# Adding a scan's states with identity matmuls, with GpSimd's products later and its decays in SBUF

## The chip, the cores and the metric

The kernel runs on one core of a Trainium2 chip. Its time is the device time of one execution in microseconds (us). Five engines work side by side, each through its own queue in order: TensorE (PE, whose weight loads are shown apart as PEld), VectorE (DVE), ScalarE (ACT), GpSimd (POOL) and SyncE (SP), which here issues most transfers. SBUF is the working memory; PSUM is a small memory of eight banks, into which PE writes its results, and which ACT and DVE can read and write[...].

## What is computed

Four layers are applied to x of shape (4, 384, 48, 48), each as x + layer(group norm of x). Layer 0 is a state-space block over the 2304 positions of each image, layers 1 to 3 are a patchwise transform with a depthwise convolution, an 11x11 depthwise convolution and a mixture of four experts. The change lies in layer 0:

```python
dt, Bm, Cm = jnp.split(x_dbl, [DT_RANK, DT_RANK + D_STATE], axis=-1)
dt = jax.nn.softplus(dt @ dt_proj_w.T + dt_proj_b)
A = -jnp.exp(A_log)

def step(h_prev, inp):
    x_t, dt_t, B_t, C_t = inp
    dA = jnp.exp(dt_t[..., None] * A)
    dBx = dt_t[..., None] * B_t[:, None, :] * x_t[..., None]
    h_new = dA * h_prev + dBx
    y_t = jnp.einsum('bds,bs->bd', h_new, C_t)
    return (h_new, y_t)
...
y = ys.transpose(1, 0, 2) + xin * D
y = y * jax.nn.silu(z)
out = y @ out_proj_w.T
```

There are 768 channels (d) and 16 states (s) for each. So y of a channel is a sum over 16 states, plus the skip term xin * D.

## The kernel before

**Tiling.** Channels lie on the 128 partitions: six tiles m = 0 to 5, taken in three pairs p. Positions of an image are cut into five chunks of 460 or 464. The smallest piece of work is a *unit*: one channel tile m, one state s, one chunk. A pair has 32 units, q = 0 to 31, the two tiles of the pair in turn, so q = 2s + m%2. There are 4 x 5 x 3 = 60 pairs and 1920 units.

**A unit** (unit(), L613 on). ACT computes the decays da = exp(dt * A) (L627) into one of two PSUM banks, tag da. POOL computes bu = u * B (L631), u being dt * x, into one of three SBUF buffers. DVE runs the recurrence along the chunk in one instruction, tensor_tensor_scan (L635), from da and bu. ACT copies the last column to carry (L640), where the next chunk's scan of the same unit starts. The states are multiplied with C (L642), and PE adds the product g to y (turned(), L591).

Two kinds of unit differ in where the scan writes. In two of three units it overwrites da in PSUM, and DVE makes the product g. In the third (q divisible by 3, 11 of a pair's 32, 660 in all) it writes into g in SBUF, and POOL makes the product in place; here these are called *Pool's units*. There are four g buffers.

**Adding up.** turned() adds g to y with four transposes by PE, each of a quarter of the columns: y stands in PSUM transposed, positions on the partitions. skip() (L604 on) begins each y: ACT computes dx = xc * D (L611) into a g buffer, and four transposes put it into y's bank. There is one bank for the even tile of a pair and one for the odd (tags y0, y1). After the pair, collect() copies y to SBUF (yt, L651) by ACT; gate(), called after units 3 and 6 of the next pair, turns yt back with four transposes into a bank pyb (L659), and DVE multiplies that with the gate silu(z) (zs, L663).

**Order.** scans() is a generator that issues units one after another, and after each unit the pieces planned for it (plan(q, piece)): the projections of the next chunk (project, project_z, expand, steps), gate, and the output projection, layer norm and residual of the chunk before (tail()). While image b is scanned, work of layers 1 to 3 for the images before it (later(), experts()) is dealt out among the units at an even rate. The instructions of each engine are then ordered by priority, which follows the order of issue, and by when their inputs and buffers are free by the compiler's own estimate; so two scans may stand in front of the first one's product. A tile's tag with bufs=n has n buffers; an instruction that needs a buffer waits until its last reader is done. Layer 0's units end at about 4920 us; the last image's layers 1 to 3 follow.

**PSUM.** Tags mm (2 banks), da (2), y0, y1 and two banks for the background work make eight.

Of the kernel before, what the change touches and what calls it, by code (L numbers as in the profile page):

```python
# [9 lines left out]
F32 = mybir.dt.float32  # L10
AF = mybir.ActivationFunctionType
ALU = mybir.AluOpType
# [4 lines left out]
P = 128  # L17
# [4 lines left out]
DI, DS, DTR, DCONV = 768, 16, 24, 4  # L22
MT = DI // P
CHUNKS = (460, 460, 460, 460, 464)
TM = max(CHUNKS)
TT = 4
# [18 lines left out]
def tile_layers(ctx: ExitStack, tc: tile.TileContext, a: dict, out: bass.AP):  # L45
    nc = tc.nc
# [16 lines left out]
    def column(ap):  # L63
        return ap.rearrange("(m p) -> p m", p=P)

    ident = const("ident", [P, P], a["c_ident"])
# [197 lines left out]
    with ExitStack() as first:  # L264
        wp = first.enter_context(tc.tile_pool(name="weights", bufs=1))
# [3 lines left out]
        def weight(name, shape, src):  # L269
            t = wp.tile(shape, F32, name=name)  # L270
            nc.scalar.dma_start(t, src)
            return t
# [18 lines left out]
        nc.vector.tensor_scalar_mul(a_neg, a_neg, -1.0)  # L291
        w_out0 = weight("w_out0", [P, MT, C], per_channel(a["L0_out_proj_wT"]))
        d_col = weight("d_col", [P, MT], column(a["L0_D"]))
        gamma = weight("gamma", [P, CT], column(a["L0_ln_gamma"]))
        beta = weight("beta", [P, CT], column(a["L0_ln_beta"]))
        carry = wp.tile([P, MT, DS], F32, name="carry")
# [26 lines left out]
        with (  # L323
# [4 lines left out]
            for ct in range(CT):  # L328
                t = pp.tile([P, HW], F32, name=f"x0_{ct}")
# [65 lines left out]
        def after(ins, other):  # L395

            tc.add_manual_dep(
                ins.ins, other.ins.name,
                mybir.DependencyInfo(
                    mybir.DependencyClass.NoSync, mybir.DependencyReason.DATA  # L400
                ),
                reason="order",
            )
# [7 lines left out]
        def scans(wk, mm):  # L411


            def bank(name):
                return mm.tile([P, 512], F32, name=name, tag="mm")
# [168 lines left out]
                    )  # L584
                    nc.gpsimd.tensor_mul(u[:, h, :n], dt[:, h, :n], c["xc"][:, 2 * p + h, :n])

            def turned(y, src, n, start, stop):

                w = n // TT
                for k in range(TT):  # L590
                    nc.tensor.matmul(  # L591
                        y[:w, bass.ts(k, P)],
                        lhsT=src[:, bass.ts(k, w)],
                        rhs=ident,
                        is_transpose=True,
                        start=start and k == 0,
                        stop=stop,
                        skip_group_check=True,
                    )

            def skip(i, p):

                (b, t), c = G[i], st[i]
                n = CHUNKS[t]  # L604
                for h in range(2):
                    m = 2 * p + h
                    y = c["y", m] = mm.tile(
                        [P, 512], F32, name=f"y{b}_{t}_{m}", tag=f"y{h}", bufs=1
                    )
                    dx = wk.tile([P, TM], F32, name=f"dx{b}_{t}_{m}", tag="g", bufs=4)  # L610
                    nc.scalar.activation(  # L611
                        dx[:, :n], c["xc"][:, m, :n], AF.Copy, scale=d_col[:, m : m + 1]
                    )  # L613
                    turned(y, dx, n, True, False)

            def unit(i, m, s):

                (b, t), c = G[i], st[i]
                n, p = CHUNKS[t], m // 2
                if m % 2 == 0:  # L620
                    bc = wk.tile([P, 2, TM], F32, name=f"bc{b}_{t}_{p}_{s}", tag="bc", bufs=4)
                    c["bct"] = bc
                    nc.sync.dma_start(bc[:, :, :n], c["bc"][:, s, :n].partition_broadcast(P))
                bc = c["bct"]
                v_ = f"{b}_{t}_{m}_{s}"
                da = mm.tile([P, 512], F32, name=f"da{v_}", tag="da")
                nc.scalar.activation(  # L627
                    da[:, :n], c["dt", p][:, m % 2, :n], AF.Exp, scale=a_neg[:, m, s : s + 1]
                )
                bu = wk.tile([P, TM], F32, name=f"bu{v_}", tag="bu", bufs=3)  # L630
                nc.gpsimd.tensor_mul(bu[:, :n], c["u", p][:, m % 2, :n], bc[:, 0, :n])  # L631
                g = wk.tile([P, TM], F32, name=f"g{v_}", tag="g", bufs=4)
                last = carry[:, m, s : s + 1]
                here = da if (2 * s + m % 2) % 3 else g
                nc.vector.tensor_tensor_scan(  # L635
                    here[:, :n], da[:, :n], bu[:, :n], last if t else nil[:, 0:1],
                    ALU.mult, ALU.add,
                )
                if t < NC - 1:
                    nc.scalar.copy(last, here[:, n - 1 : n])  # L640
                eng = nc.vector if here is da else nc.gpsimd
                eng.tensor_mul(g[:, :n], here[:, :n], bc[:, 1, :n])  # L642
                turned(c["y", m], g, n, False, s == DS - 1)

            def collect(i, p):
                (b, t), c = G[i], st[i]
                w = CHUNKS[t] // TT
                for h in range(2):
                    m = 2 * p + h
                    yt = c["yt", m] = wk.tile([P, 512], F32, name=f"yt{b}_{t}_{m}", tag="yt")  # L650
                    nc.scalar.copy(yt[:w, :], c["y", m][:w, :])  # L651

            def gate(i, m):
                (b, t), c = G[i], st[i]
                n = CHUNKS[t]
                w = n // TT
                ps = bank(f"pyb{b}_{t}_{m}")
                for k in range(TT):
                    nc.tensor.transpose(  # L659
                        ps[:, bass.ts(k, w)], c["yt", m][:w, bass.ts(k, P)], ident[:w, :w]  # L660
                    )
                zm = c["zs"][:, m, :n]
                nc.vector.tensor_tensor(zm, ps[:, :n], zm, ALU.mult)  # L663

            def out_proj(i, k):
                (b, t), c = G[i], st[i]
# [52 lines left out]

            def tail(i):  # L720

                yield lambda: gate(i, MT - 2)
                yield lambda: gate(i, MT - 1)
                for k in range(TT):
                    yield lambda k=k: out_proj(i, k)
                yield lambda: layer_norm(i)
                for ct in range(CT):
                    yield lambda ct=ct: residual(i, ct)
# [9 lines left out]
            for i, (b, t) in enumerate(G):  # L738
                todo = {}

                def plan(q, piece):
                    todo.setdefault(q, []).append(piece)

                more = i + 1 if i + 1 < len(G) else None
                if more is not None:
                    if t == NC - 1:
                        fold(b + 1, 0)
                    load(more)
                if t == 0 and b:
                    plan(12, lambda: fold(b, 1))  # L750
                if i:
                    for k, piece in enumerate(tail(i - 1)):
                        plan(2 + 2 * k, piece)
                for j in range(MT):
                    if more is not None:
                        plan(1 + 4 * j, lambda j=j: project(more, j))
                    plan(15 + 2 * j, lambda j=j: project_z(i, j))
                plan(28, lambda: gates(more, i))
                if more is not None:
                    plan(38, lambda: expand(more))  # L760
                    plan(76, lambda: steps(more, 0))
                if b + 1 < NB and t < CT:
                    plan(46, lambda: image_stats(b + 1, t, 0))
                    plan(66, lambda: image_stats(b + 1, t, 1))
                if b + 1 < NB and t == CT:
                    plan(50, lambda: image_norm(b + 1))
                for p in range(MT // 2):
                    if p:
                        for h in range(2):
                            plan(2 * DS * p + 3 + 3 * h, lambda m=2 * p - 2 + h: gate(i, m))  # L770
                    if p < MT // 2 - 1:
                        plan(2 * DS * p + DS, lambda p=p: steps(i, p + 1))
                for p in range(MT // 2):
                    skip(i, p)
                    for q in range(2 * DS):
                        unit(i, 2 * p + q % 2, q // 2)
                        for piece in todo.pop(2 * DS * p + q, []):
                            piece()
                        yield b, t, 2 * DS * p + q
                    collect(i, p)  # L780
                assert not todo
            for piece in tail(len(G) - 1):
                piece()

# [572 lines left out]
```

## Time and profile before

| | us |
|---|---|
| three runs, median (lowest to highest) | 5813.99 (5811.21 to 5818.36) |
| the profiled execution, its own time | 5822.38 |
| its span, first to last instruction | 5820.6 |
| mean of one decay exp, L627 | 0.645 |
| mean of one scan, L635 | 1.17 |
| mean of one bu, L631, and one product on POOL, L642 | 1.17, 1.16 |
| mean of one product on DVE, L642 | 0.626 |
| transposes into y from g, count and PE busy | 7680, 1346.3 |
| matmul of 384 columns, L673, count and PE busy | 960, 344.2 |

The profile is one execution, recorded by instruction. A row of it names the line, the engine, the operation, output and inputs, and gives the busy time, the mean duration in ns and the idle time of the engine just before, with what ended it. "A L1 <- B L2: t, n, max" means that engine A, at line 1, stood idle for t us in n places until line 2 of B was done. Matmul ends are modelled, and matmuls overlap, so busy time over count is closer to what one costs in a dense stretch than the mean duration is.

### The profile page before, as it was taken

To read this page: it belongs to the slowest core of one execution; us is meant where nothing else is said; L and a number is where in the kernel's file an instruction comes from. 1 tells how busy PE (TensorE), PEld (TensorE's weight loads), DVE (VectorE), ACT (ScalarE), POOL (GpSimd) and SP (SyncE) were. 2 spreads that over 40 slices of the span, in tenths; PEclk is the share of its full clock that TensorE was granted. 3 is DMA by queue.
4 is the path that set the end of the run, shared out by engine and by line. 5 is a ranking of instruction groups with operands and counts; after the bars stand their busy time and mean duration, and the time that the engine had idled before them with its cause. 6 is when DMAs were issued, how large, how long until landed. Compare 5 with 4: busy or idle time off the path is not lost. (4 is left out here: it accounts for less than half of the span.)

```text
span 5820.6 us, 78509 instructions
## 1 busy us (share of the span) xinstructions
PE 4897.0 (84%) x27796; PEld 3787.9 (65%) x27796; DVE 4014.5 (69%) x5653; ACT 3053.3 (52%) x6658; POOL 3110.4 (53%) x2795
## 2 busy tenths in 40 slices
PE   6677667778778898999867798999967698899999
PEld 3544444544456665889544676789744486789999
DVE  5888878889888787767788678666788767451110
ACT  3555555555566665555555576555555575345321
POOL 3877877765657677646464457555554556000000
PEclk9688778878789898999978699899978699899999
DMA  4344334333334335334333235333332334311100
GB/s 135 124 132 133 123 124 134 126 106 117 103 128 140 108 126 177 125 97 123 108 107 106 90 125 180 98 102 115 112 101 91 106 109 131 113 36 47 57 22 26
DMA packets 396048, 634.78 MB, mean 109 GB/s; under 512 B 32373, under 2 KB 386789, under 8 KB 392190
## 3 DMA queue, kind: packets, MB, share of 16 engines
q1 hardware_dynamic: 382148, 618.58, 33.5%
q10 hardware_dynamic: 13498, 11.11, 0.6%
q8 instruction: 220, 3.60, 0.3%
q14 instruction: 182, 1.49, 0.1%
HBM read 571.80 MB, written 57.80 MB: 108 GB/s over the span
## 5 line engine op out<-in xcount | busy, mean ns | idle before, releaser
L631 POOL TENSOR_TENSOR bu<-u,bc 128x460 f32<-128x460 f32 (+1 forms) x1920 | 2217.5, 1168 | 1348.8 <-DVE g L635 748.0
L591 PE MATMUL y<-ident,g 128*115 128x128 f32 (+1 forms) x7680 | 1346.3, 316 | 637.2 <-POOL g L642 539.8
L591 PEld LDWEIGHTS y<-ident,g 128*115 128x115 f32 (+1 forms) x7680 | 1110.5, 199 | 998.7 <-POOL g L642 686.2
L627 ACT ACTIVATE da<-dt,a_neg 128x460 f32<-128x460 f32 (+1 forms) x1920 | 1220.8, 645 | 667.3 <-DVE g L642 585.2
L635 DVE TENSOR_TENSOR_SCAN da<-da,carry,bu 128x460 f32<-128x460 f32 (+1 forms) x1008 | 1160.6, 1170 | 194.7 <-ACT da L627 155.6
L642 POOL TENSOR_TENSOR g<-g,bc 128x460 f32<-128x460 f32 (+1 forms) x660 | 765.9, 1160 | 268.2 <-DVE g L635 127.3
L642 DVE TENSOR_TENSOR g<-da,bc 128x460 f32<-128x460 f32 (+1 forms) x1260 | 771.1, 626 | 159.8 <-ACT carry L640 85.4
L635 DVE TENSOR_TENSOR_SCAN g<-da,carry,bu 128x460 f32<-128x460 f32 (+1 forms) x528 | 616.9, 1168 | 150.4 <-PE y L591 65.3
L1142 PE MATMUL ph<-xe,w 128*128 128x144 f32 x4608 | 624.8, 289 | 4.4 <-ACT hr L1150 3.9
L1160 PE MATMUL pout<-hr,w 128*128 128x144 f32 x4608 | 616.1, 287 | 0.0
L1142 PEld LDWEIGHTS ph<-xe,w 128*128 128x128 f32 x4608 | 591.1, 192 | 24.9 <-issue 10.9
L1160 PEld LDWEIGHTS pout<-hr,w 128*128 128x128 f32 x4608 | 584.8, 190 | 14.8 <-issue 7.9
L1001 PE MATMUL pc<-band,row 128*128 128x162 f32 (+14 forms) x3456 | 506.3, 297 | 3.8 <-DVE x L1019 3.5
L1001 PEld LDWEIGHTS pc<-band,row 128*128 128x128 f32 x3456 | 478.5, 205 | 20.9 <-DVE x L1019 6.9
L640 ACT COPY carry<-da 128x1 f32<-128x1 f32 x1008 | 158.7, 159 | 581.0 <-DVE da L635 575.9
L1150 ACT ACTIVATE hr<-ph,nb 128x144 f32<-128x144 f32 x768 | 235.6, 377 | 409.8 <-PE ph L1142 409.7
L881 DVE SCALAR_TENSOR_TENSOR dw<-pad,w_dw,dw 128x384 f32<-128x384 f32 x576 | 342.5, 610 | 12.9 <-ACT pad L869 9.3
L673 PE MATMUL po<-w_out,zs 128*115 128x384 f32 (+1 forms) x960 | 344.2, 500 | 4.3 <-DVE xc L504 3.5
L635 DVE TENSOR_TENSOR_SCAN da<-da,nil,bu 128x460 f32<-128x460 f32 x252 | 289.4, 1168 | 83.2 <-ACT da L627 65.9
L487 PE MATMUL pin<-xch,w_inx 128*128 128x463 f32 (+2 forms) x720 | 329.7, 586 | 7.6 <-DVE dt L582 5.4
L515 PE MATMUL pinz<-xch,w_inz 128*128 128x460 f32 (+1 forms) x720 | 317.9, 574 | 16.0 <-DVE xc L504 7.3
L1171 DVE SCALAR_TENSOR_TENSOR xe<-pout,b_sum,xe 128x144 f32<-128x144 f32 x192 | 58.7, 359 | 340.3 <-PE pout L1160 340.3
(173 smaller groups left out, 5355.6 us busy)
## 6 DMA issues: line engine op xcount, KB each, us to landing
bc<-bcd SPq DMA_DIRECT2D x768, 460.0 KB, 3.7
bc<-bcd SPq DMA_DIRECT2D x192, 464.0 KB, 3.6
xs<-x1d SPq DMA_DIRECT2D x24, 576.0 KB, 4.1
x2d<-xs SPq DMA_DIRECT2D x24, 576.0 KB, 3.0
x<-x2d SPq DMA_DIRECT2D x12, 1152.0 KB, 8.8
x3d<-x SPq DMA_DIRECT2D x12, 1152.0 KB, 4.6
xg<-x3d SPq DMA_DIRECT2D x24, 576.0 KB, 3.9
xe<-x3d SPq DMA_DIRECT2D x64, 216.0 KB, 2.6
```

The costliest lines, as they stand in the source:

```text
L487: nc.tensor.matmul(ps[:, lo : halo + n], lhsT=w_inx[:, k, bass.ts(j, P)], rhs=c["x"][:, k, lo : halo + n], start=k == 0, stop=k == CT - 1,)
L515: nc.tensor.matmul(ps[:, :n], lhsT=w_inz[:, k, bass.ts(j, P)], rhs=c["x"][:, k, DCONV - 1 : DCONV - 1 + n], start=k == 0, stop=k == CT - 1,)
L591: nc.tensor.matmul(y[:w, bass.ts(k, P)], lhsT=src[:, bass.ts(k, w)], rhs=ident, is_transpose=True, start=start and k == 0, stop=stop, skip ...
L627: nc.scalar.activation(da[:, :n], c["dt", p][:, m % 2, :n], AF.Exp, scale=a_neg[:, m, s : s + 1])
L631: nc.gpsimd.tensor_mul(bu[:, :n], c["u", p][:, m % 2, :n], bc[:, 0, :n])
L635: nc.vector.tensor_tensor_scan(here[:, :n], da[:, :n], bu[:, :n], last if t else nil[:, 0:1], ALU.mult, ALU.add,)
L642: eng.tensor_mul(g[:, :n], here[:, :n], bc[:, 1, :n])
L673: nc.tensor.matmul(ps[:w, :C], lhsT=c["zs"][:, m, bass.ts(k, w)], rhs=w_out0[:, m, :], start=m == 0, stop=m == MT - 1,)
L881: nc.vector.scalar_tensor_tensor(v, src, w_dw[:, ct, k : k + 1], v, ALU.mult, ALU.add)
L1001: nc.tensor.matmul(d["acc2"][:, : BANDS[k] * W].rearrange("p (h w) -> p h w", w=W)[:, lo - edges[k] : hi - edges[k], xlo:xhi], lhsT=d["row ...
L1142: nc.tensor.matmul(ps[:, bass.ts(m, EB)], lhsT=d["w1"][:, e, k, bass.ts(m, P)], rhs=d["x", s][:, k, :], start=k == 0, stop=k == CT - 1,)
L1160: nc.tensor.matmul(d["o"][:, bass.ts(m, EB)], lhsT=d["w2"][:, e, k, bass.ts(m, P)], rhs=d["h", s, e][:, k, :], start=e == 0 and m == 0 and ...
```

## The change

PE no longer turns y. summed() adds one product to y in its own layout with a single matmul against the identity, ident, so y stands with channels on partitions. The skip term is one matmul of xc against d_diag, a diagonal matrix of D for each tile, which six ACT instructions make at the start; it is issued after unit 16 of the pair. The first sum that is issued to a bank starts it, and the seventeenth ends it. collect() and the way back are gone; gate() multiplies y from its bank, and is called after the first unit of the next pair, or of the next chunk. The other pieces of tail() come three units earlier.

In Pool's units da is now a buffer in SBUF (tag das, two buffers); the other units keep the two PSUM banks to themselves. There are six g buffers. In the other units the product stands ahead of carry's copy. The sum of a Pool product is put off: it is issued after two sums of other units, or at the pair's end, and an ordering edge without a wait keeps it behind them on PE.

```diff
+        d_diag = wp.tile([P, MT, P], F32, name="d_diag")
+        for m in range(MT):
+            nc.scalar.activation(d_diag[:, m, :], ident, AF.Copy, scale=d_col[:, m : m + 1])
...
-            def turned(y, src, n, start, stop):
-
-                w = n // TT
-                for k in range(TT):
-                    nc.tensor.matmul(
-                        y[:w, bass.ts(k, P)],
-                        lhsT=src[:, bass.ts(k, w)],
-                        rhs=ident,
-                        is_transpose=True,
-                        start=start and k == 0,
-                        stop=stop,
-                        skip_group_check=True,
-                    )
-
-            def skip(i, p):
+            def summed(i, m, lhsT, src):
 
                 (b, t), c = G[i], st[i]
                 n = CHUNKS[t]
-                for h in range(2):
-                    m = 2 * p + h
-                    y = c["y", m] = mm.tile(
-                        [P, 512], F32, name=f"y{b}_{t}_{m}", tag=f"y{h}", bufs=1
-                    )
-                    dx = wk.tile([P, TM], F32, name=f"dx{b}_{t}_{m}", tag="g", bufs=4)
-                    nc.scalar.activation(
-                        dx[:, :n], c["xc"][:, m, :n], AF.Copy, scale=d_col[:, m : m + 1]
-                    )
-                    turned(y, dx, n, True, False)
+                if ("y", m) not in c:
+                    c["y", m] = mm.tile(
+                        [P, 512], F32, name=f"y{b}_{t}_{m}", tag=f"y{m % 2}", bufs=1
+                    )
+                    c["terms", m] = 0
+                c["terms", m] += 1
+                return nc.tensor.matmul(
+                    c["y", m][:, :n],
+                    lhsT=lhsT,
+                    rhs=src,
+                    start=c["terms", m] == 1,
+                    stop=c["terms", m] == DS + 1,
+                    skip_group_check=True,
+                )
+
+            def skip(i, p):
+
+                (b, t), c = G[i], st[i]
+                for m in (2 * p, 2 * p + 1):
+                    summed(i, m, d_diag[:, m, :], c["xc"][:, m, : CHUNKS[t]])
...
-                da = mm.tile([P, 512], F32, name=f"da{v_}", tag="da")
+                slow = (2 * s + m % 2) % 3 == 0
+                da = (
+                    wk.tile([P, TM], F32, name=f"das{v_}", tag="das", bufs=2)
+                    if slow else mm.tile([P, 512], F32, name=f"da{v_}", tag="da")
+                )
...
-                g = wk.tile([P, TM], F32, name=f"g{v_}", tag="g", bufs=4)
+                g = wk.tile([P, TM], F32, name=f"g{v_}", tag="g", bufs=6)
                 last = carry[:, m, s : s + 1]
-                here = da if (2 * s + m % 2) % 3 else g
+                here = g if slow else da
...
-                if t < NC - 1:
-                    nc.scalar.copy(last, here[:, n - 1 : n])
-                eng = nc.vector if here is da else nc.gpsimd
-                eng.tensor_mul(g[:, :n], here[:, :n], bc[:, 1, :n])
-                turned(c["y", m], g, n, False, s == DS - 1)
-
-            def collect(i, p):
-                (b, t), c = G[i], st[i]
-                w = CHUNKS[t] // TT
-                for h in range(2):
-                    m = 2 * p + h
-                    yt = c["yt", m] = wk.tile([P, 512], F32, name=f"yt{b}_{t}_{m}", tag="yt")
-                    nc.scalar.copy(yt[:w, :], c["y", m][:w, :])
+                late = c.setdefault("late", [])
+                if here is da:
+                    nc.vector.tensor_mul(g[:, :n], here[:, :n], bc[:, 1, :n])
+                    if t < NC - 1:
+                        nc.scalar.copy(last, here[:, n - 1 : n])
+                    ins = summed(i, m, ident, g[:, :n])
+
+                    c["since"] = c.get("since", 0) + 1
+                    if late and (c["since"] >= 2 or (m % 2 and s == DS - 1)):
+                        after(late.pop(0)(), ins)
+                else:
+                    if t < NC - 1:
+                        nc.scalar.copy(last, here[:, n - 1 : n])
+                    nc.gpsimd.tensor_mul(g[:, :n], here[:, :n], bc[:, 1, :n])
+                    late.append(lambda: summed(i, m, ident, g[:, :n]))
+                    c["since"] = 0
 
             def gate(i, m):
                 (b, t), c = G[i], st[i]
                 n = CHUNKS[t]
-                w = n // TT
-                ps = bank(f"pyb{b}_{t}_{m}")
-                for k in range(TT):
-                    nc.tensor.transpose(
-                        ps[:, bass.ts(k, w)], c["yt", m][:w, bass.ts(k, P)], ident[:w, :w]
-                    )
                 zm = c["zs"][:, m, :n]
-                nc.vector.tensor_tensor(zm, ps[:, :n], zm, ALU.mult)
+                nc.vector.tensor_tensor(zm, c["y", m][:, :n], zm, ALU.mult)
...
                 if i:
+                    for m in (MT - 2, MT - 1):
+                        plan(0, lambda m=m: gate(i - 1, m))
                     for k, piece in enumerate(tail(i - 1)):
-                        plan(2 + 2 * k, piece)
+                        plan(3 + 2 * k, piece)
...
-                            plan(2 * DS * p + 3 + 3 * h, lambda m=2 * p - 2 + h: gate(i, m))
+                            plan(2 * DS * p, lambda m=2 * p - 2 + h: gate(i, m))
                     if p < MT // 2 - 1:
                         plan(2 * DS * p + DS, lambda p=p: steps(i, p + 1))
+                    plan(2 * DS * p + DS, lambda p=p: skip(i, p))
                 for p in range(MT // 2):
-                    skip(i, p)
                     for q in range(2 * DS):
                         unit(i, 2 * p + q % 2, q // 2)
...
-                    collect(i, p)
```

More of the change, by code (lines that the diff above doesn't have):

```diff
@@ L585, in steps @@
                     nc.gpsimd.tensor_mul(u[:, h, :n], dt[:, h, :n], c["xc"][:, 2 * p + h, :n])
-            def turned(y, src, n, start, stop):
-                w = n // TT
-                for k in range(TT):
-                    nc.tensor.matmul(
-                        y[:w, bass.ts(k, P)],
-                        lhsT=src[:, bass.ts(k, w)],
-                        rhs=ident,
-                        is_transpose=True,
-                        start=start and k == 0,
-                        stop=stop,
-                        skip_group_check=True,
-                    )
+            def summed(i, m, lhsT, src):
+                (b, t), c = G[i], st[i]
+                n = CHUNKS[t]
+                if ("y", m) not in c:
+                    c["y", m] = mm.tile(
+                        [P, 512], F32, name=f"y{b}_{t}_{m}", tag=f"y{m % 2}", bufs=1
+                    )
+                    c["terms", m] = 0
[8 more added lines that the diff above has]
+                )
             def skip(i, p):
                 (b, t), c = G[i], st[i]
-                n = CHUNKS[t]
-                for h in range(2):
-                    m = 2 * p + h
-                    y = c["y", m] = mm.tile(
-                        [P, 512], F32, name=f"y{b}_{t}_{m}", tag=f"y{h}", bufs=1
-                    )
-                    dx = wk.tile([P, TM], F32, name=f"dx{b}_{t}_{m}", tag="g", bufs=4)
-                    nc.scalar.activation(
-                        dx[:, :n], c["xc"][:, m, :n], AF.Copy, scale=d_col[:, m : m + 1]
-                    )
-                    turned(y, dx, n, True, False)
+                for m in (2 * p, 2 * p + 1):
+                    summed(i, m, d_diag[:, m, :], c["xc"][:, m, : CHUNKS[t]])
             def unit(i, m, s):
@@ L720, in tail @@
             def tail(i):
-                yield lambda: gate(i, MT - 2)
-                yield lambda: gate(i, MT - 1)
                 for k in range(TT):
@@ L779, in scans @@
                         yield b, t, 2 * DS * p + q
-                    collect(i, p)
                 assert not todo
+            for m in (MT - 2, MT - 1):
+                gate(len(G) - 1, m)
             for piece in tail(len(G) - 1):
```

## The prediction

> **What bounds the kernel now.** I read the page first, for its busy shares and slices, then busy time by stage, then VectorE's waits, then the order of time in two stretches. The page:
>
> ```profile
> PE 4897.0 (84%) x27796; PEld 3787.9 (65%) x27796; DVE 4014.5 (69%) x5653; ACT 3053.3 (52%) x6658; POOL 3110.4 (53%) x2795
> ...
> DVE  5888878889888787767788678666788767451110
> ...
> POOL 3877877765657677646464457555554556000000
> ```
>
> Pool works in the first 34 of 40 slices: that is the scan stage, where every unit of the change lies. Its stages, by windows (span, PE, PE weight loads, DVE, ACT, POOL, PE clock, DMA):
>
> ```profile
> 250.00:1150.00 900.00, 645.48 (x2773) 438.43 (x2771) 755.69 (x957) 481.52 (x1017) 693.71 (x619) 0.80 0.41 129
> 1150.00:4930.00 3780.00, 3223.67 (x18066) 2446.64 (x18064) 2894.02 (x4001) 2157.12 (x4667) 2279.25 (x2037) 0.88 0.37 117
> 4930.00:5821.00 891.00, 866.96 (x6358) 798.58 (x6356) 199.83 (x464) 302.70 (x745) 4.30 (x14) 0.97 0.15 49
> ```
>
> The first line is image 0 after its start: DVE is 84% busy and Pool 77%. The second is images 1 to 3: DVE 77%, PE 85%, Pool 60%, no engine full, so the time lies in what they do to each other. The last 891 us has no scan and stays as it is. By the same view in steps of 250 us, PE is busy 93 to 99% from 2250 to 2750 and from 3750 to 4250, and is the bound there. What VectorE waits for in the scan stage (total us, times, longest):
>
> ```profile
> DVE da L635 <- ACT da L627: 221.6, 210, 9.1
> DVE g L642 <- ACT carry L640: 85.4, 118, 9.1
> DVE g L635 <- PE y L591: 71.9, 51, 4.0
> ...
> DVE zs L663 <- PE pyb L659: 46.4, 29, 6.5
> ...
> DVE g L642 <- PE y L591: 36.4, 30, 2.5
> ...
> DVE da L635 <- ACT carry L640: 34.4, 28, 3.9
> ```
>
> The first is a scan that lacks its decays: exp has two PSUM banks, and a bank is free only after VectorE's product. Where nothing disturbs it, image 0 runs like this (start, us, engine, line):
>
> ```profile
> 569.80 1.18 DVE L635 TENSOR_TENSOR_SCAN g<-da,carry,bu 128x460 f32<-128x460 f32 x1 [0.23 <-issue]
> ...
> 570.90 2.22 DVE L635 TENSOR_TENSOR_SCAN da<-da,carry,bu 128x460 f32<-128x460 f32 x2
> ...
> 572.17 1.16 POOL L642 TENSOR_TENSOR g<-g,bc 128x460 f32<-128x460 f32 x1
> ...
> 573.03 1.16 DVE L642 TENSOR_TENSOR g<-da,bc 128x460 f32<-128x460 f32 x2
> ...
> 573.29 3.57 POOL L631 TENSOR_TENSOR bu<-u,bc 128x460 f32<-128x460 f32 x3
> ...
> 574.42 1.17 DVE L635 TENSOR_TENSOR_SCAN g<-da,carry,bu 128x460 f32<-128x460 f32 x1 [0.23 <-issue]
> ```
>
> Three units, one of them Pool's, in 574.42 - 569.80 = 4.62 us, with VectorE idle 0.23 and Pool's four products taking 4.7: both are full, side by side. Note that Pool computes straight through the scan at 574.42 (its products last to 576.86).
>
> **What the skill says.** "SBUF — State Buffer", Who interferes with whom: a VectorE instruction with two SBUF inputs contends with a GpSimd instruction that reads SBUF; the pair of ports is an exclusive lock, and the loser blocks fully. The kernel before has such instructions only in tiny sizes, and its trace agrees:
>
> ```profile
> 2799.32 1.16 POOL L631 TENSOR_TENSOR bu<-u,bc 128x460 f32<-128x460 f32 x1
> 2799.77 0.72 DVE L105 TENSOR_TENSOR dev<-mv,mean 128x3 f32<-128x3 f32 x1
> ```
>
> A 3-element subtraction, 0.16 us in the median of 16, takes 0.72 and ends at 2800.49, as Pool's product does (2800.48). Another, at 791.74, takes 2.05 us and ends with the second of two products that Pool ran back to back: VectorE gets the lock when Pool has a gap. "PSUM — Partial Sum Buffer", PSUM bank collisions raise a hardware error: two engines may not be on one bank together; so carry's copy and VectorE's product on the same bank follow one another (85.4 us above). "Perfetto Trace Analysis", Optimizing Scalar/DVE Operations: VectorE's access overhead is about 60 ns on SBUF against 125 on PSUM, ScalarE's 93 against 51; no row here shows the same operation from both.
>
> **The change part by part**, against the profiled execution's 5822.4 us (span 5820.6; 8 us, 0.14%, over the median 5814.0).
>
> (1) Decays of Pool's units to SBUF. 660 scans (528 + 132 in the rows) now read da and bu both from SBUF, so each takes the lock for its 1.11 us (spacing in a run of scans) and must first find Pool idle. In the undisturbed stretch above the cycle can't be shorter than Pool's 4.6 plus 1.1 = 5.7 us, instead of 4.62. A chunk of image 0 takes 200 us (lnm at 316, 515, 712, 922, 1116), with Pool busy 154; 33 locked scans add 37, so the lock is wanted 191 us of 200. Part of that is Pool's old idle time: it waited 93.5 us of the 900 for these very scans to free a bu buffer. I take 0.6 us a scan on the path: 165 x 0.6 = +100. In the other images Pool is 60% busy; half of a 1.16 us product times 0.6 is 0.35, and since a scan's end is what starts Pool's next product, and products run in pairs, 0.45; VectorE has slack for 0.4 of it: 495 x 0.45 x 0.6 = +135. Together +235. Bounds: 0 if Pool is always in a gap, 660 x 1.16 = +765 if every scan waits for a whole product. Scan and exp themselves: by the skill's figures an estimate of 660 x 65 ns = -43 on VectorE and +28 on ScalarE, which is half idle; I take 0.
>
> (2) Two banks for two thirds of the units, product ahead of carry's copy, six g buffers. These can remove da waits (222 and 36 + 16 of the smaller rows), carry's 85 + 34, y's 72 + 36: 501 in all. Some 49 lie in the 900 us of image 0 (the same view cut to it), the rest in images 1 to 3. Some return: carry now waits for the product 0.6 us longer and ScalarE's next exp stands behind it. In the PE-bound stretches (64 of the 222 in 2250 to 2750) VectorE has no use for them. I take 45%: -225; bounds -70 and -450.
>
> (3) States added with the identity. Four transposes a unit go, one 460-column matmul with one weight load comes. In 2250 to 2750 the transposes cost 113.4 us for 195 units, 0.58 each; 384 columns of po cost 344/960 = 0.36, so 460 cost 0.43, with the gap 0.48: 0.10 x 1920 = 190 us of PE. The transposes back (73 + 18) go, and the skip's 8 a pair become 2 (106 to 120 x 0.5 = 60). This counts only where PE is the bound, about a quarter of the stage: -70. Elsewhere PE's 540 us of waits for Pool's product shrink, since two other units' sums go first, without anyone waiting for PE. Bounds -130 and 0. yt's copies (120 x 0.59) and dx (120 x 0.68) leave ScalarE, 52% busy: 0.
>
> (4) gate reads y itself, after the next pair's first unit and not at units 3 and 6. It waits for the last sums, among them the Pool product of unit 30, and behind it on VectorE stand the next pair's scans; on PE the next pair's first sum waits for gate, with six g to fill meanwhile. 60 pairs x 1.5 us = +90, less the 46 on pyb that go: +45; bounds 0 and +150. Skip moves to the middle of a pair, where nothing waits for it; the tail's projections and their stores on SP come three units earlier: 0. Six d_diag activations stand ahead of ScalarE's later weight DMAs and wait for d_col's landing: +5.
>
> Sum: 235 - 225 - 70 + 45 + 5 = -10, with two terms of over 200 us that don't know of each other. They aren't alike in certainty. The lock is in the trace in both its lengths and strikes every one of 660 scans; the waits in (2) are what this order of instructions shows, and in-order queues pass such a wait on. With 0.35 in place of 0.45 for (2), -175, and the lock's second half (Pool, held up 1.1 us, is then late for the next scan) at +20, the sum is **+60: 5880**, and from the median **about 5870**.
>
> **The rivals.**
> A, the lock slightly outweighs: 5870, own range 5830 to 5980; 0.43.
> B, the other side: the banks were the knot. With da never missing, VectorE arrives at the Pool unit's scan when Pool has used up its three bu and idles, as at 580.90, where Pool started only at 582.15, released by that very scan. The lock then costs 0.15 us a scan (+100), (2) gives -225 and (3) -70, (4) +45 and 5: -145, or 5670. It decides where a wait is under 0.35 us a scan. For it: Pool waits 748 us for just these scans. Against: the 4.62 us cycle, in which Pool never pauses. 0.35.
> C, the lock starves: Pool, behind, always has a product ready, a scan waits 1 us and Pool's lateness stops the fast scans: 660 x 0.8 = +530 in place of 235, less the 195 of A's other terms: about 6150. For it 791.74; against it the 60% of Pool in later images; 0.14.
> D, everything falls into slack of images 1 to 3: 5814; 0.08.
>
> **How the numbers follow.** A measurement of this kernel tells 0.2% from no change (12 us). Faster: B and little else, 0.36; same 0.08; slower: A and C, 0.56. The range reaches from B's lower part, where (1) is near its lower bound, to C's near side: 5620 to 6130; A's own stands above.
>
> **What would show it.** The scan of Pool's units reads longer than 1.17 us in the mean (1.5 or more), some over 2, ending with a Pool product; Pool's products rest during those scans. Waits da <- exp fall below 100 us, carry's to nothing. L663's wait moves to y, over 50 us. PE's matmul on y: about 0.43 to 0.6 us, 2040 of them. If those scans stay at 1.17 us with Pool busy beside them, the lock is wrong and B or better follows; if da's waits stay, (2) is.

## The result, and the profile after

| | before | after |
|---|---|---|
| median, us (lowest to highest, 4 runs each) | 5816.17 (5811.21 to 5818.50) | 5947.07 (5943.06 to 5965.93) |
| ratio, 95% interval | | 1.0233 [1.0209, 1.0256] |
| the profiled execution, span | 5820.6 | 5964.1 |

The change makes the kernel 131 us slower. The forecast was slower by some 57 us (5870): the direction came, at more than twice the size.

Three rows of the page before (line, engine, operation, count, busy us, mean ns, idle before):

```profile
L631 POOL TENSOR_TENSOR bu<-u,bc 128x460 f32<-128x460 f32 (+1 forms) x1920 | 2217.5, 1168 | 1348.8 <-DVE g L635 748.0
L591 PE MATMUL y<-ident,g 128*115 128x128 f32 (+1 forms) x7680 | 1346.3, 316 | 637.2 <-POOL g L642 539.8
...
L635 DVE TENSOR_TENSOR_SCAN g<-da,carry,bu 128x460 f32<-128x460 f32 (+1 forms) x528 | 616.9, 1168 | 150.4 <-PE y L591 65.3
```

The page of the kernel after, first its busy shares, then the rows of the same three kinds of instruction, and of the scans whose decays stayed in PSUM:

```profile
PE 5312.1 (89%) x23236; PEld 3357.7 (56%) x23236; DVE 4213.7 (71%) x5653; ACT 2956.5 (50%) x6425; POOL 3341.8 (56%) x2795
...
L634 POOL TENSOR_TENSOR bu<-u,bc 128x460 f32<-128x460 f32 (+1 forms) x1920 | 2408.2, 1270 | 1248.5 <-DVE da L638 571.0
L600 PE MATMUL y<-g,ident 128*128 128x460 f32 (+1 forms) x3840 | 1860.3, 604 | 355.8 <-DVE g L644 332.4
...
L638 DVE TENSOR_TENSOR_SCAN da<-da,carry,bu 128x460 f32<-128x460 f32 (+1 forms) x1008 | 1154.6, 1168 | 130.0 <-POOL bu L634 67.3
...
L638 DVE TENSOR_TENSOR_SCAN g<-das,carry,bu 128x460 f32<-128x460 f32 (+1 forms) x528 | 782.3, 1482 | 85.9 <-PE y L600 76.4
```

Three things are to be seen. The scans of Pool's units (g<-das) take 1.48 us in the mean, where the other scans stay at 1.17. Pool's bu takes 1.27 in the mean in place of 1.17, 191 us over all 1920. And the sums into y are **3840** matmuls for 1920 products: a matmul in f32 is two instructions here, while a transpose was one (7680 for 1920 x 4). PE's work on y went up from 1346 to 1860 us; it had been forecast to fall.

The wait that was to go has gone, and others stand in its place. VectorE's waits in the scan stage, after:

```profile
DVE g L644 <- PE y L600: 178.9, 113, 7.4
DVE g L638 <- PE y L600: 105.0, 72, 7.1
...
DVE da L638 <- POOL bu L634: 82.3, 79, 2.4
...
DVE da L638 <- ACT da L630: 53.4, 60, 2.6
...
DVE zs L663 <- PE y L600: 26.9, 23, 2.4
```

Scans that write da wait 53 us for their decays instead of 222. But VectorE now waits 284 us until PE has read a g buffer (108 before), and those scans wait 82 us for a bu (7 before).

How a long scan comes about can be read in image 0, in order of time (start, us):

```profile
572.70 1.16 POOL L634 TENSOR_TENSOR bu<-u,bc 128x460 f32<-128x460 f32 x1 [8.10 <-DVE g L638]
573.07 1.77 DVE L638 TENSOR_TENSOR_SCAN g<-das,carry,bu 128x460 f32<-128x460 f32 x1
...
573.82 1.97 POOL L655 TENSOR_TENSOR g<-g,bc 128x460 f32<-128x460 f32 x1
```

The scan starts inside Pool's product, which ends at 573.86, and ends 0.98 us later, at 574.84. Pool's next product starts at 573.82 and takes 1.97 us where it took 1.16 before: it sat out the scan. A blocked instruction shows as a long one, not as an idle engine. Of the 660 scans of this kind, 418 began while Pool was computing: 1.66 us in the mean. The 242 that found Pool idle took 1.17, in mean and median, and none over 1.19: two SBUF inputs alone don't make a scan longer. This is the lock that the Trainium skill tells of in "SBUF — State Buffer", Who interferes with whom, and this trace shows it in both directions.

The time by image, read from the profiled executions (that of after lies 19 us above its median). An image ends where the last of its five layer-norm rows (lnm) starts, and the next begins there; image 0 begins with the span, and "rest" is what follows image 3:

| us | image 0 | 1 | 2 | 3 | rest |
|---|---|---|---|---|---|
| before | 1116 | 1173 | 1358 | 1302 | 871 |
| after | 1140 | 1179 | 1415 | 1358 | 872 |

Images 2 and 3 lose 56 us each, images 0 and 1 only 24 and 6. The windows of image 2, before and after (stretch, then PE, PE weight loads, DVE, ACT, POOL, PE clock):

```profile
2290.00:3648.00 1358.00, 1186.63 (x6948) 923.79 (x6947) 1000.35 (x1398) 759.84 (x1663) 778.84 (x697) 0.90 0.37 116
```

```profile
2320.00:3735.00 1415.00, 1305.38 (x5788) 831.58 (x5788) 1037.68 (x1398) 738.34 (x1601) 818.95 (x697) 0.95 0.35 111
```

PE is busy 119 us longer, though at a higher clock, and stands at 92% of the longer stretch. DVE and POOL grow by 37 and 40 us, as the lock would have it.

### The profile page after: what moved, and what is told of

Same layout as the page of the kernel before. It is cut to its first block, busy times and chain, and to the rows that moved or that the text cites. A ratio compares the mean times of both kernels' runs of the same rounds, so it can differ in the third digit from the quotient of the medians.

```text
span 5964.1 us, 68781 instructions
## 1 busy us (share of the span) xinstructions
PE 5312.1 (89%) x23236; PEld 3357.7 (56%) x23236; DVE 4213.7 (71%) x5653; ACT 2956.5 (50%) x6425; POOL 3341.8 (56%) x2795
## 5 line engine op out<-in xcount | busy, mean ns | idle before, releaser
L634 POOL TENSOR_TENSOR bu<-u,bc 128x460 f32<-128x460 f32 (+1 forms) x1920 | 2408.2, 1270 | 1248.5 <-DVE da L638 571.0
L600 PE MATMUL y<-g,ident 128*128 128x460 f32 (+1 forms) x3840 | 1860.3, 604 | 355.8 <-DVE g L644 332.4
L600 PEld LDWEIGHTS y<-g,ident 128*128 128x128 f32 x3840 | 715.4, 204 | 1074.6 <-DVE g L644 575.5
L655 POOL TENSOR_TENSOR g<-g,bc 128x460 f32<-128x460 f32 (+1 forms) x660 | 783.3, 1187 | 262.7 <-DVE g L638 149.7
L630 ACT ACTIVATE da<-dt,a_neg 128x460 f32<-128x460 f32 (+1 forms) x1260 | 808.2, 647 | 186.0 <-DVE g L644 160.6
L638 DVE TENSOR_TENSOR_SCAN g<-das,carry,bu 128x460 f32<-128x460 f32 (+1 forms) x528 | 782.3, 1482 | 85.9 <-PE y L600 76.4
L1002 PEld LDWEIGHTS pc<-band,row 128*128 128x128 f32 x3456 | 464.7, 197 | 93.7 <-issue 46.8
L630 ACT ACTIVATE das<-dt,a_neg 128x460 f32<-128x460 f32 (+1 forms) x660 | 444.3, 674 | 110.1 <-DVE g L638 103.6
L1002 PE MATMUL pc<-band,row 128*128 128x162 f32 (+14 forms) x3456 | 476.2, 289 | 15.8 <-ACT row L991 10.8
L654 ACT COPY carry<-g 128x1 f32<-128x1 f32 x528 | 100.7, 191 | 526.4 <-DVE g L638 519.2
```

Source lines behind the costliest of these rows:

```text
L600: return nc.tensor.matmul(c["y", m][:, :n], lhsT=lhsT, rhs=src, start=c["terms", m] == 1, stop=c["terms", m] == DS + 1, skip_group_check=True,
L630: nc.scalar.activation(da[:, :n], c["dt", p][:, m % 2, :n], AF.Exp, scale=a_neg[:, m, s : s + 1])
L638: nc.vector.tensor_tensor_scan(here[:, :n], da[:, :n], bu[:, :n], last if t else nil[:, 0:1], ALU.mult, ALU.add,)
L655: nc.gpsimd.tensor_mul(g[:, :n], here[:, :n], bc[:, 1, :n])
L1002: nc.tensor.matmul(d["acc2"][:, : BANDS[k] * W].rearrange("p (h w) -> p h w", w=W)[:, lo - edges[k] : hi - edges[k], xlo:xhi], lhsT=d["row ...
```

## The experiments

Two theories for the loss: **the lock** (decays in SBUF), and **PE** (a sum is two instructions). A third question was why the waits that the forecast counted as gain gave so little. All were timed against the kernel before on the same chip.

**1. Decays back in PSUM, the rest as after.**

```diff
-                da = (
-                    wk.tile([P, TM], F32, name=f"das{v_}", tag="das", bufs=2)
-                    if slow else mm.tile([P, 512], F32, name=f"da{v_}", tag="da")
-                )
+                da = mm.tile([P, 512], F32, name=f"da{v_}", tag="da")
```

> The kernel after, with the decays of Pool's units back in the two PSUM banks and all else as after. Lock theory (two SBUF inputs make these scans wait for Pool and Pool for them): the scans of Pool's units go back from 1.48 to 1.17 us, bu from 1.27 to 1.17, image 0 loses its 24 us, and the time falls by 80 to 150 us, to 5800 to 5870. PE theory (a sum is two matmul instructions, 0.97 us of PE a unit in place of the 0.48 forecast): images 2 and 3 stay 50 us a piece over before, and the time stays at 5900 to 5950, more if the scans wait for decays again.

Measured: 5765.22 us, 0.9923 [0.9904, 0.9941] of before. That is 182 us under the kernel after, and under before too; the time even passed the lower end of what the lock theory gave. Images 2 and 3 (1391 and 1344 us) stay 33 and 42 us over before, where the PE theory said 50; images 0 and 1 (1057 and 1107) are 59 and 66 under it. The rows of this run:

```profile
L631 POOL TENSOR_TENSOR bu<-u,bc 128x460 f32<-128x460 f32 (+1 forms) x1920 | 2216.7, 1167 | 1346.2 <-DVE g L635 627.1
...
L635 DVE TENSOR_TENSOR_SCAN g<-da,carry,bu 128x460 f32<-128x460 f32 (+1 forms) x528 | 617.3, 1169 | 133.1 <-PE y L600 67.0
```

Scan and bu are back at 1.17. VectorE's wait for decays is back as well, 236 us, and the kernel is faster all the same.

**2. Decays of Pool's units in SBUF, alone, in the kernel before.** The inverse edit of run 1, on before.py's unit().

> The kernel before, with the decays of Pool's units in SBUF and nothing else changed. Lock theory: slower than before by 60 to 150 us (5880 to 5970), scans of Pool's units near 1.48 us, image 0 slower by 20 or more. Bank theory (two banks were the knot): waits of da on exp go from 222 to under 80 us and the time is 5700 to 5816.

Measured: 5972.25 us, 1.0266 [1.0249, 1.0283]: 155 us slower, 2 us over the lock theory's range, and slower in all four images (1177, 1212, 1395, 1328).

```profile
L639 DVE TENSOR_TENSOR_SCAN g<-das,carry,bu 128x460 f32<-128x460 f32 (+1 forms) x528 | 761.6, 1442 | 69.0 <-PE y L591 61.8
...
DVE da L639 <- ACT da L631: 199.9, 181, 7.6
```

The scans of Pool's units take 1.44 us. What the bank theory said did not come: alone, the edit leaves the wait for decays at 200 us. It fell to 53 only in the kernel after, with the order, the six g buffers and the sums beside it; which of them that takes was not tried.

**3. Sums over half the columns, the rest as after.** It leaves terms out of half of y, and shows what sums that cost PE less would be worth.

```diff
+                w = n if c["terms", m] == 1 else n // 2
                 return nc.tensor.matmul(
-                    c["y", m][:, :n],
+                    c["y", m][:, :w],
                     lhsT=lhsT,
-                    rhs=src,
+                    rhs=src[:, :w],
```

> The kernel after, with every sum into y but a bank's first taken over the first half of the columns, so the other half of y lacks these terms; waits and buffers as after, PE's work on y about halved to the 0.48 us a unit that was forecast. PE theory: about 900 us less of PE work, images 2 and 3 fall below before, time 5700 to 5800. Lock theory alone: 5920 to 5947.

Measured: 5726.33 us, 0.9849 [0.9833, 0.9866], 221 under the kernel after. Images 2 and 3 take 1329 and 1276 us, below before, as the PE theory says.

```profile
L601 PE MATMUL y<-g,ident 128*128 128x230 f32 (+2 forms) x3840 | 1266.2, 455 | 578.2 <-DVE g L645 559.7
```

PE's busy time on y fell less than by half, to 1266 us. A sum still costs 1266/1920 = 0.66 us, more than the 0.48 that had been forecast; that is enough to bring the kernel below before, with the lock in place.

**4. Both: decays in PSUM and sums over half the columns** (the edits of runs 1 and 3).

> The kernel after, with the decays of Pool's units back in PSUM and every sum but a bank's first over half of the columns (the other half of y lacks these terms). If lock and PE's cost are two separate losses that add up: 5765 less the 221 us that halving brought with the lock in place, 5520 to 5580. If the lock had been hiding part of PE's cost, or the other way round: 5600 to 5700.

Measured: 5579.43 us, 0.9595 [0.9579, 0.9611], at the upper edge of the first range. With sums halved the lock costs 5726 - 5579 = 147 us, with whole sums 182; halving brings 186 us without the lock, 221 with it. The two losses are separate, and add up but for about 35 us. PE's row on y is close to run 3's (1255.6 us).

**5. Order and six buffers alone, in the kernel before.**

```diff
+                if here is da:
+                    nc.vector.tensor_mul(g[:, :n], here[:, :n], bc[:, 1, :n])
                 if t < NC - 1:
                     nc.scalar.copy(last, here[:, n - 1 : n])
-                eng = nc.vector if here is da else nc.gpsimd
-                eng.tensor_mul(g[:, :n], here[:, :n], bc[:, 1, :n])
+                if here is g:
+                    nc.gpsimd.tensor_mul(g[:, :n], here[:, :n], bc[:, 1, :n])
```

and bufs=6 for the tag g.

> The kernel before, with VectorE's product ahead of carry's copy and six g buffers, sums by transposes, decays in PSUM. If carry's 120 us and y's 108 us of VectorE's waits were on the path: 5700 to 5770. If in-order queues pass them on: 5800 to 5816.

Measured: 5781.44 us, 0.9944 [0.9928, 0.9961]: 36 us gained, between the two expectations. Where the rest went is in VectorE's waits:

```profile
DVE da L635 <- ACT da L627: 282.2, 231, 8.8
...
DVE g L640 <- PE y L591: 50.4, 44, 2.9
...
DVE g L635 <- PE y L591: 44.6, 19, 5.3
DVE g L635 <- ACT da L627: 40.6, 37, 4.9
...
DVE g L635 <- ACT carry L642: 10.0, 20, 1.9
DVE da L635 <- ACT carry L642: 8.5, 9, 1.9
```

The product's wait for carry (85 us) is no longer listed and the scans' are 18.5 in place of 34. But scans wait for decays 61 us longer than before (282 against 222). Two more g buffers took only 13 us from the waits for PE, 108 to 95.

**6. The same, and Pool's sums late.** turned() returns its last matmul, and the transposes of a Pool product are issued behind two other units', as in the kernel after.

> The kernel before, with VectorE's product ahead of carry's copy, six g buffers, and the transposes of Pool's products put off behind two other units' as in the kernel after. If PE's 478 us of waits for Pool's product cost time: 5720 to 5760, against 5781 without the delay. If nobody waits for PE there: 5775 to 5790.

Measured: 5793.33 us, 0.9956 [0.9941, 0.9971], no gain over run 5, and 3 us over the range that had been given for no gain. The rows of run 5 and of this run:

```profile
L591 PE MATMUL y<-ident,g 128*115 128x128 f32 (+1 forms) x7680 | 1356.2, 319 | 572.3 <-POOL g L644 478.1
```

```profile
L591 PE MATMUL y<-ident,g 128*115 128x128 f32 (+1 forms) x7680 | 1301.8, 317 | 414.9 <-DVE g L641 370.0
```

PE's 478 us of waits for Pool's product fall to 43 (its largest wait on y is now for VectorE's product, 370 us), and the whole got no faster. By image it isn't nothing: 1117, 1124, 1372, 1299 us, where run 5 has 1105, 1172, 1344, 1291, so image 1 gains 48 us and the others lose as much. Why is open. With transposes, the later products bring no time over the whole kernel.

**7. One instruction a sum.** Decays in PSUM; g and the identity are float32r, and a sum is then one matmul.

```diff
-                g = wk.tile([P, TM], F32, name=f"g{v_}", tag="g", bufs=6)
+                g = wk.tile([P, TM], F32R, name=f"g{v_}", tag="g", bufs=6)
...
-                    ins = summed(i, m, ident, g[:, :n])
+                    ins = summed(i, m, ident_r, g[:, :n])
```

(likewise for the late sums; ident_r is a float32r copy of ident.)

> The kernel after, with the decays of Pool's units in PSUM, and g and the identity as float32r, so that a sum is one matmul[...] in place of two. PE theory: PE's work on y falls below half of 1838 us and images 2 and 3 fall below before: 5450 to 5580. If the second instruction cost nothing: 5765.

Measured: 5517.45 us, 0.9478 [0.9461, 0.9494]. The row of the sums:

```profile
L603 PE MATMUL y<-g,ident_r 128*128 128x460 f32 (+1 forms) x1920 | 914.6, 549 | 632.7 <-DVE g L644 626.7
```

Half the instructions and half the busy time of run 1 (1838.5 us), with all columns in place. The time falls by 248 us against run 1, as the PE theory says; that is what the second instruction cost. Image by image 1045, 1103, 1268 and 1244 us: against run 1 (1057, 1107, 1391, 1344) nearly all of it in images 2 and 3, where PE is the bound.

**8. By image: sums with the identity in images 0 and 1, transposes in 2 and 3.** Decays in PSUM, order and six buffers as in run 5; each form keeps its own skip and gate.

```diff
+                    if b >= 2:
+                        turned(c["y", m], g, n, False, s == DS - 1)
+                        return
                     ins = summed(i, m, ident, g[:, :n])
```

> Decays in PSUM, product ahead of carry's copy, six g; identity sums in images 0 and 1, where PE has room, and transposes with collect and the way back in images 2 and 3, where PE is the bound. PE theory: images 0 and 1 as in the run with decays in PSUM (1057 and 1107 us), 2 and 3 as in the run with the six g buffers (1344 and 1291): 5650 to 5690. If it isn't PE's room by image that matters: 5740 to 5790.

Measured: 5698.48 us, 0.9803 [0.9779, 0.9826], 8 us over the expected range. Images 1061, 1108, 1360, 1304: the first two are run 1's, the last two are those of the kernel before, and the 25 us that run 5 gained in them did not come along; why is open. It keeps the sums in f32 and is faster than both kernels.

## Why the prediction was wrong

The runs split the change into three steps that add up (medians, us):

| step | forecast | measured |
|---|---|---|
| order and six g (before to run 5) | in (2): -175, with the banks' relief | -36 |
| sums, gate, skip, late (run 5 to run 1) | (3), (4), (5): -20 | -16 |
| decays in SBUF (run 1 to after) | (1): +255 | +182, with the banks' relief |
| sum | +60 | +130 |

**(1) was right in mechanism, and near in size as far as can be told.** The lock was read from two tiny subtractions in the trace of before, and what was said of it came: 1.48 us in the mean (forecast 1.5 or more), the longest over 3, Pool waiting in turn, image 0 slower. From run 1 to after the four images lose 83, 72, 24 and 14 us; the forecast had +100 for image 0 and +155 for the others. The estimate for scan and exp themselves (-43 and +28) did not come in its first part: a scan that found Pool idle took the same 1.17 us as with decays in PSUM. Exp took 0.674 us to SBUF against 0.647, or 18 us over 660. The measured +182 is the lock less what the freed banks gave back. Those two can't be taken apart with these runs: a lock-free way to a third bank was not tried. Only their sum has a number: +155 in the kernel before, +182 with the sums, +147 with halved sums.

**(2) failed: "With 0.35 in place of 0.45 for (2), -175".** It took a share of 501 us of listed waits as gain. Order and buffers stand for 228 of the 501, and so for some 80 of the 175; they brought 36. Run 5 shows what came instead: of the 228 us 115 went, and the waits for decays rose from 274 to 323. A bank is free only when both product and carry's copy are done, whichever comes first, so the exp behind them comes no sooner; this fits the kernel, but no run isolates it. The forecast had seen that carry then waits longer with exp behind it, and still counted 35%. The waits for decays did go in the kernel after, from 274 to 55 us, but only together with the lock, and (1) and (2) jointly are +146 where +80 was forecast. That is 66 of the missing 70 us.

**(3) failed in its mechanism, and its sum came right by luck.** PE's work on y was to fall by 190 us and rose by 514. "Bounds -130 and 0" rested on 0.48 us a sum, worked out from 384-column matmuls as busy over count. The count of that row was the clue: 960 for 20 chunks x 4 x 6 = 480 products, two instructions each.

```profile
L673 PE MATMUL po<-w_out,zs 128*115 128x384 f32 (+1 forms) x960 | 344.2, 500 | 4.3 <-DVE xc L504 3.5
```

A sum costs 1860/1920 = 0.97 us of PE, against 0.70 for the transposes. The gain lay where it was not looked for, in the images with room on PE: run 1 against run 5 is 48 us better in image 0 and 64 in image 1, and 47 and 53 us worse in images 2 and 3. They cancel: the intervals of runs 1 and 5 overlap. Of the parts of this step only the late sums were tried alone (run 6, with transposes: image 1 gains 48 us, image 0 loses 12); which of the others (no copy and way back, gate earlier, skip later) makes the gain was not tried. At the forecast's price of a sum the step would have been far from -20: run 7, with one instruction of 0.48 us, is 264 us under run 5. "Slower" itself hangs on that price: run 3, with cheaper sums and the lock in place, is 91 us under before. Taking away either the lock (run 1) or the price of the sums (run 3) gives a kernel faster than before, and the forecast had priced only the lock: that the direction came is in part luck too.

**(4), (5)**: gate waits 27 us for y (over 50 had been forecast) where 46 was spent on pyb, so the +45 for it was too high. The start's +5 can't be told from other differences of image 0.

Of the rivals, B needs the scan to find Pool idle; 418 of 660 did not. C overstated the starving: the waits of scans for a late bu came to 82 us, not to a stop. That PE's cost of a sum doubles was on no list.

## What to carry to other kernels

An operand moved from PSUM to SBUF can give a VectorE instruction its second SBUF input. These scans then shut GpSimd out and were shut out by it: count such instructions before moving a buffer, and price each with the time that both engines lose. Price a matmul per product, not per row of the profile: check the row's count against the loop's. A list of waits is not a list of gains; with carry's wait out of the way, run 5 waits longer for decays.

## What was not expected of the hardware

A 460-column f32 matmul shows as two MATMUL instructions, 0.97 us of PE busy a product, the float32r one as one, 914.6/1920 = 0.48 us; the f32 transposes stay at one each, 1346.3/7680 = 0.18 us.

The granted clock of PE rose with the change: mean 0.880 before, 0.944 after, 0.954 in run 1, and 0.873 in run 3, 0.852 in run 7, where PE had less to do. PE's busy time for the same instruction is longer where the clock is lower. By image, the clock, and PE's busy time on y per instruction, times the clock (us):

| | image 0 | 1 | 2 | 3 |
|---|---|---|---|---|
| before, clock | 0.800 | 0.855 | 0.897 | 0.898 |
| before, time x clock | 0.152 | 0.153 | 0.149 | 0.151 |
| after, clock | 0.919 | 0.941 | 0.946 | 0.953 |
| after, time x clock | 0.452 | 0.450 | 0.456 | 0.451 |
| run 3, clock | 0.765 | 0.852 | 0.890 | 0.905 |
| run 3, time x clock | 0.277 | 0.275 | 0.274 | 0.274 |

In each kernel the product of the two hardly moves while the clock does. At full clock a sum would thus cost PE 2 x 0.45 = 0.90 us and the four transposes 4 x 0.15 = 0.60, an estimate from this table. In run 3 the slower clock took back a part of what was saved: y's busy time in image 0 went from 511 to 378 us, 26%, at 0.765 in place of 0.919; at equal clock it would be 39%, by 0.277 against 0.452. That this is still less than the 47% of columns left out is not explained here. Why the clock was lower where PE had less to do was not tested.
